# Where quantised tiles stand among VectorE's work: pinned steps, other homes for the tiles, gating in four portions

## The chip, the cores and the metric

The kernel runs on one core of a Trainium2 chip. The core has five engines that work side by side, each with a queue of its own that it works through in order: TensorE (PE in the profile; its weight loads are listed as PEld), VectorE (DVE), ScalarE (ACT), GpSimd (POOL) and SyncE (SP, which here only issues DMA transfers). An engine whose next instruction waits for another engine stands still, and everything behind that instruction in its queue stands with it. The metric is the device time of one execution in microseconds; the time of a kernel is the median of several executions.

## The reference, cut to what matters

Two batches of 4096 tokens with 512 channels pass through two layers, each of which adds an attention part and a feed-forward part to x. In layer 0 the feed-forward part is a product of two tensors that are first quantised: every run of 32 numbers in a row shares a scale, and each number divided by the scale is rounded to a 6-bit grid.

```python
xn = _layernorm(x)
# layer 0, attention: x1 = xn@w1.T+b; conv over 3 tokens, silu, a linear recurrence over all
# tokens (16 states a channel); v = silu(xn@v1.T+b); result (ssm * v) @ w2.T + b
# layer 0, ffn:
xq, xs = _mx_quantize(xn)          # scales = max|block of 32| / 7.5 ; q = nearest on grid
wq, ws = _mx_quantize(weight)
ffn = (xq * xs) @ (wq * ws).T + bias
x = x + attention + ffn
xn = _layernorm(x)
# layer 1, attention: q, k = relu(xn@Wq.T+bq), relu(xn@Wk.T+bk); v = xn@Wv.T+bv;
#   linear attention over 16 heads (sums of k and of k*v over all tokens), + xn, layernorm
# layer 1, ffn: sigmoid(xr@W_r.T) * (relu(xk@W_k.T)**2 @ W_v.T), xr, xk mixes with the token before
x = x + attention + ffn
```

## The kernel before, in words

A block is 512 tokens (T); a batch has NB = 8 of them, and a block has four tiles of 128 tokens (TJ = 4). Channels come in four chunks of 128 (CC = 4). Everything is float32; larger products are made from seven smaller ones instead of eight, with sums and differences made by VectorE and GpSimd beforehand.

The order of the work, with the times at which it lies in the profiled execution:

1. The w1 loops (to about 460 us): `projected` for all 16 blocks makes x1 and v by w1 and v1 and runs the convolution; tables for the recurrence are made beside it. Blocks 13 and 14 go together, by `projected_pair`.
2. The recurrence over tokens (460 to 570), which leaves its result y in memory.
3. For each batch: `mixed`, the w2 loops (570 to 905 for batch 0, from 1430 for batch 1). For each block, "gating" (`gated`) loads four chunks of y and of v, transposes y (L638) and multiplies (L639); TensorE multiplies the gated block by w2 and the quantised tiles by the quantised weight `w_d` into the same bank. Blocks 0 and (in batch 0) 1 go by `branch` and `x1_of` (matmuls L743, sums L751), the later ones by `x1_by_seven` (matmuls L787, sums L805). Then follow the layer norm of the result, its transposed form xnT and the keys of layer 1 (L902, L903).
4. `outer_sums` (905 to 982 us for batch 0), the product of keys and x over all tokens, one block in about 12 us: VectorE makes four differences (L951) and GpSimd eight (L943), TensorE multiplies (L971).
5. `pairs` (982 to 1175): q and the feed-forward keys for two blocks at a time (matmuls L1081).
6. `layer1` (1175 to 1430): attention, the second feed-forward product and the output, block by block. It calls `at_block(i, half)` in each block, a place for work that belongs to the next batch.

**A quantised tile** is 128 tokens, 64 of them in all, and four more for the weight. `quantised` is a generator in four steps: load xq (a DMA on SyncE's queue, L456); rescale it (four ScalarE activations, L136), take the scales (VectorE: L187, L188, L192) and multiply (GpSimd, L193); round by a conversion to FP8 (VectorE, L201) and multiply by the scales (GpSimd, L202); transpose (VectorE, L464) and, unless the tile goes straight to a place on the chip, store it. `stepped(tiles)` is what the loops call at chosen places: it takes the first tile in the list a step further, and the second as well once the first has done more than two. A tile therefore goes through in about two calls. Its buffer xq comes from the pool "yv" of eight buffers, which y and v of the gating use too, unless it is given another home.

Where the tiles stand before:

- the w1 loops (`beside`): blocks 0 to 5 of batch 0 (24 tiles) and the weight's four;
- the w2 loops (`tiles` in `mixed`): blocks 6 and 7 of the batch at hand (8 tiles), stepped in the branch loop, in `x1_of(0)`, in `x1_by_seven` and in the loop of the keys;
- the outer sums of batch 0 (`early`): blocks 4 and 5 of batch 1 (8 tiles), one call at every second item;
- the pairs of batch 0 (`later`): blocks 1 to 3 of batch 1 (12 tiles), one call at each of the places that `seven` offers;
- layer 1 of batch 0 (`ahead`): block 0 of batch 1 (4 tiles).

The gating of block 0 of batch 1 stands in layer 1 of batch 0 too, all four chunks at `at_block(7, 0)`.

**What sets the order.** The program is written as a sequence of steps, but a scheduler of the framework places each engine's instructions, from what each depends on and its own view of when they will be ready. So an engine's queue can differ from the order in which the instructions are written. The call `tc.keep_in_program_order(ins)` holds an instruction behind the one that was traced before it on its engine; it changes the place in the queue and adds no instruction.

Of the kernel before, what the change touches and what calls it, by code (L numbers as in the profile page):

```python
# [13 lines left out]
ALU = mybir.AluOpType  # L14
# [3 lines left out]
P = 128  # L18
# [26 lines left out]
def block_kernel(ctx: ExitStack, tc: tile.TileContext, a: dict, out: bass.AP):  # L45
# [132 lines left out]
    def laid_normalised(y, mv, rescaled=rescaled):  # L178

        for h in range(QC):  # L180
            part = y.rearrange("p (c h q) -> p c h q", h=QC, q=QB)[:, :, h, :]
            rescaled(part, part, mv[:, h, :])

    def mx_scaled(y):

        s = small.tile([P, NQ], F32, tag="mx_s", name="mx_s", bufs=6)
        nc.vector.tensor_reduce(s, by_block(y), AX.X, ALU.max, apply_absolute_value=True)  # L187
        nc.vector.tensor_scalar(  # L188
            s, s, (1.0 / 7.5) / GRID, 1e-30 / GRID, ALU.mult, ALU.max
        )  # L190
        rs = small.tile([P, NQ], F32, tag="mx_rs", name="mx_rs")
        nc.vector.reciprocal(rs, s)  # L192
        nc.gpsimd.tensor_tensor(  # L193
            by_block(y), by_block(y), rs.unsqueeze(2).to_broadcast([P, NQ, QB]), ALU.mult
        )
        return s

    def mx_rounded(y, s):

        q = small.tile([P, D], FP8, tag="mx_q", name="mx_q")  # L200
        nc.vector.tensor_scalar(q, y, -LOWER * GRID, None, ALU.add, saturate=False)  # L201
        nc.gpsimd.tensor_tensor(  # L202
            by_block(y), by_block(q), s.unsqueeze(2).to_broadcast([P, NQ, QB]), ALU.mult
        )
# [184 lines left out]
            :, 2 * j : 2 * j + 2, half * 2 * P : (half + 1) * 2 * P  # L389
        ]  # L390

    def projected_pair(work, m, xa, xb, before, sums):

        x_work = lambda name: work.tile([P, T], F32, tag="x", name=name, bufs=10)
        ts = [None] + [[x_work("t") for _ in range(2)] for _ in range(3)]
# [38 lines left out]
        for half in range(2):  # L434
            seven(
                two_quarters(half), sums[half], lambda k: xa[:, k, :], lambda k: xb[:, k, :], ts,
                ("acc", "mm", "tr"), partial(put, half), lambda: None,
                held=[x_work("held") for _ in range(4)],
            )
        return x1s[1]  # L440

    def quantised_weight(o):
        y = yv.tile([P, D], F32, tag="yv", name="w_y")
        nc.sync.dma_start(out=y, in_=a["ffn_w"][o])
        yield
        s = mx_scaled(y)
        yield
        mx_rounded(y, s)
        yield
        nc.vector.transpose(wd[:, :, o * P : (o + 1) * P], y)  # L450
        yield

    def quantised(n, j, dst, temp, home=None):

        xq = home("xq") if home else yv.tile([P, D], F32, tag="yv", name="xq")
        nc.sync.dma_start(out=xq, in_=a["xi"][n * TJ + j])  # L456
        yield
        laid_normalised(xq, mvi[:, :, n, j, :])
        scales = mx_scaled(xq)
        yield  # L460
        mx_rounded(xq, scales)
        yield
        xd = dst().rearrange("p c t -> p (c t)") if dst else temp()
        nc.vector.transpose(xd, xq)  # L464
        if not dst:
            nc.sync.dma_start(out=xqd[n, j], in_=xd)
        yield
# [173 lines left out]
    def mixed(b, z0, xds, xnTs, mvs, w2, wk, outer):  # L641
# [19 lines left out]
        def at(time, do):  # L661
            events[max(time, clock[0])].append(do)

        tiles = [
            quantised(b * NB + m, j, None, t2q) for m in (NB - 2, NB - 1) for j in range(TJ)
        ]

        def xnT_of(i):
# [64 lines left out]
        def x1_of(i):  # L733

            xt, z = xts[i], zs.pop(i)
            for j in range(TJ):
# [15 lines left out]
                nc.sync.dma_start(out=xd1[b * NB + i, j * P : (j + 1) * P], in_=xt[:, j, :])  # L752
                tick()
                gate(i + 1, j)
                if i == 0:
                    stepped(tiles)
            measured_x1(i, xt)

        def halves_of(z, xd):
# [107 lines left out]
        for i in range(plain):  # L867

            pos[i] = [bank(("mm", "tr")[i]) if j < 2 else acc() for j in range(TJ)]
            for j in range(TJ):  # L870
                branch(i, j, pos[i][j])
                if i == 0:
                    tick()
                stepped(tiles)
        x1_of(0)
        w_sums = [weight_sums(quarters(w)) for w in (wd, w2)]
        xd_read(2)
# [324 lines left out]
    def layer1(b, xrs, mvs, kvx, wts, at_block):  # L1202
# [143 lines left out]
        loaded(0)  # L1346
        for i in range(NB + 1):
            steps = receptance(i) if i < NB else iter(())
            if i < NB:
                at_block(i, 0)  # L1350
            if i + 1 < NB:
                loaded(i + 1)
            for j in range(TJ):
                next(steps, None)
                if i:
                    added(i - 1, j)
                if j < TJ - 1:
                    next(steps, None)
                if i < NB:
                    attention(i, j)  # L1360
                    if j == 1:
                        at_block(i, 1)
            if i < NB:
                normalised(i)

# [6 lines left out]
    with tc.tile_pool(name="tab", bufs=1) as tab:  # L1372
# [3 lines left out]
        with pool("a", 2) as work, pool("pm", 1) as pm:  # L1376
# [32 lines left out]
            for u in range(2):  # L1409
# [17 lines left out]
                    m, j, partial(homes[m], j) if m in homes else None,  # L1427
                    lambda: work.tile([P, D], F32, tag="xe", name="c"),
                )
                for m in range(NB - 2)  # L1430
                for j in range(TJ)
            ]
            beside += [quantised_weight(o) for o in range(CC)]
# [11 lines left out]
            while n < NK:  # L1445
                if n == PAIRED:

                    xi = laid(work, n + 2)
                    x1 = projected_pair(work, n, xnT, xnT_b, x1, sums)
# [53 lines left out]
    for b in range(B):  # L1503
# [5 lines left out]
        early, later = [], []  # L1509
        if b + 1 < B:  # L1510
            tile_of = lambda m, j, home=None: quantised((b + 1) * NB + m, j, None, t2q, home)
            early = [tile_of(m, j, t2) for m in (4, 5) for j in range(TJ)]
            later = [tile_of(m, j) for m in range(1, 4) for j in range(TJ)]
        for n, item in enumerate(outer):
            if n % 2:
                stepped(early)
            gt = item
        while early:
# [89 lines left out]
```

## Time and profile before

| | |
|---|---|
| runs shown, us | 2279.46, 2282.87, 2285.77 |
| median, us | 2282.87 |
| profiled execution, us | 2286.98 |
| its span, us | 2285.2 |
| mean granted clock of TensorE | 0.997 |
| TensorE busy, us | 2233.7 (98% of the span), 8032 matmuls |
| VectorE busy, us | 1589.7 (70%), 3115 instructions |
| ScalarE busy, us | 1052.0 (46%), 2066 instructions |
| GpSimd busy, us | 543.5 (24%), 576 instructions |

The profile is of one execution; "L639" is line 639 of the kernel before. Groups of instructions are named `out<-in` by the tiles that they write and read. An idle time is put down to what ended it: `[8.64 <-DVE x L805]` is 8.64 us in which the engine stood, until VectorE's instruction of line 805 that writes x was done. The granted clock is the share of full speed that TensorE was given in a stretch. A stretch in the windows view shows the busy time of TensorE, of its weight loads, of VectorE, ScalarE and GpSimd, then the granted clock, the share of the DMA engines and GB/s.

### The profile page before, as it was taken

How to read it: one execution, taken by the hardware profiler on the slowest of the kernel's cores; microseconds unless marked ns; L12 is line 12 of the kernel's file. 1: busy time of each engine (PE TensorE's matmuls, PEld its weight loads, DVE VectorE, ACT ScalarE, POOL GpSimd, SP SyncE). 2: the span in 40 equal slices, each digit the busy share in tenths (PEclk: the TensorE clock that was granted, in tenths of full speed). 3: DMA queues.
4: the chain of work that ended last, by engine and by line, in shares of the span. 5: the costliest groups of instructions: out<-in, count | busy, mean ns of one | idle time of the engine just before them, and what ended most of it. 6: DMA issues, size and time to landing. Idle time of an engine off the chain costs nothing. (4 is left out here: it accounts for less than half of the span.)

```text
span 2285.2 us, 25778 instructions
## 1 busy us (share of the span) xinstructions
PE 2233.7 (98%) x8032; PEld 1337.0 (59%) x8032; DVE 1589.7 (70%) x3115; ACT 1052.0 (46%) x2066; POOL 543.5 (24%) x576
## 2 busy tenths in 40 slices
PE   7999999999999999999999999899999999999999
PEld 3443344455467676854456665567676864456665
DVE  6798847655676764588678878776664455558877
ACT  5777884546232234367763332222132256653332
POOL 0124300011342224722021111423233600001111
PEclk9999999999999999999999999999999999999999
DMA  7865543389876557523276788756556412266876
GB/s 252 278 222 157 164 153 114 117 265 320 293 233 221 176 177 224 188 102 137 112 268 164 213 214 244 238 176 218 172 165 208 161 49 81 97 226 155 218 211 167
DMA packets 304571, 431.15 MB, mean 189 GB/s; under 512 B 60081, under 2 KB 121521, under 8 KB 303409
## 3 DMA queue, kind: packets, MB, share of 16 engines
q1 hardware_dynamic: 262096, 330.91, 44.0%
q10 hardware_dynamic: 29088, 67.12, 7.6%
q0 software_dynamic: 13248, 31.46, 7.4%
q8 instruction: 64, 1.05, 0.2%
q14 instruction: 75, 0.61, 0.1%
HBM read 249.42 MB, written 148.53 MB: 174 GB/s over the span
## 5 line engine op out<-in xcount | busy, mean ns | idle before, releaser
L165 PE MATMUL p_acc<-w_W_v,t 128*128 128x512 f32 x512 | 230.2, 594 | 1.2 <-DMA t<-kd 1.2
L1318 POOL DMA_DIRECT2D x<-row_beta x64 | 55.9, 898 | 427.9 <-DVE den L1300 220.3
L165 PEld LDWEIGHTS p_acc<-w_W_v,t 128*128 128x128 f32 x512 | 96.4, 190 | 102.2 <-issue 95.3
L193 POOL TENSOR_TENSOR xq<-xq,mx_rs 128x512 f32<-128x512 f32 x64 | 71.4, 1117 | 330.0 <-DVE mx_rs L192 168.8
L136 ACT ACTIVATE xq<-xq,mvi 128x128 f32<-128x128 f32 x256 | 109.0, 484 | 83.1 <-DMA xq<-in_xi 68.8
L860 POOL TENSOR_TENSOR ksum<-ksum,k 128x512 f32<-128x512 f32 x62 | 84.8, 1367 | 257.0 <-ACT k L903 249.9
L903 ACT ACTIVATE k<-k 128x512 f32<-128x512 f32 x64 | 40.3, 630 | 209.6 <-DVE k L902 180.1
L485 DVE SCALAR_TENSOR_TENSOR xc<-x,col_conv_w,xc 128x512 f32<-128x512 f32 x128 | 99.1, 796 | 41.7 <-ACT x L346 23.6
L165 PE MATMUL p_acc<-xnT,w_w_w 128*128 128x512 f32 x224 | 103.8, 607 | 5.1 <-ACT x L364 2.3
L118 ACT ACTIVATE rs_s<-rs_v 128x4 f32<-128x4 f32 (+1 forms) x41 | 8.4, 206 | 211.9 <-DVE rs_v L116 211.7
L787 PE MATMUL p_mm<-w_sums,t 128*128 128x256 f32 x416 | 96.9, 387 | 8.6 <-DVE x L805 8.6
L165 PE MATMUL p_acc<-xnT,w_v_w 128*128 128x512 f32 x224 | 101.2, 594 | 3.2 <-ACT v L380 3.1
L165 PE MATMUL p_acc<-w_Wk,xnT 128*128 128x512 f32 x224 | 101.5, 593 | 1.2 <-DVE xnT L697 1.2
L165 PE MATMUL p_tr<-w_Wk,xnT 128*128 128x512 f32 x224 | 100.9, 592 | 0.0
L131 DVE BATCH_NORM_STATS2 st<-x 128x6 f32<-128x512 f32 x128 | 83.7, 677 | 22.7 <-DMA x<-in_x 21.8
L136 ACT ACTIVATE xi<-xi,mvi 128x128 f32<-128x128 f32 x208 | 89.3, 483 | 11.1 <-DMA xq<-in_xi 3.7
L787 PE MATMUL p_acc<-w_sums,t 128*128 128x256 f32 x416 | 94.2, 379 | 0.0
L787 PEld LDWEIGHTS p_mm<-w_sums,t 128*128 128x128 f32 x416 | 80.9, 195 | 21.0 <-DVE x L805 9.3
L136 ACT ACTIVATE t<-t,mvj 128x128 f32<-128x128 f32 x224 | 87.6, 479 | 3.5 <-DMA ktd<-k 3.1
L971 PE MATMUL p_acc<-t,t 128*128 128x256 f32 x384 | 88.1, 379 | 0.0
L202 POOL TENSOR_TENSOR xq<-mx_q,mx_s 128x512 f32<-128x512 fp8e4 x64 | 72.3, 1130 | 64.5 <-DVE mx_q L201 39.2
L1081 PE MATMUL p_acc<-x,w_sums 128*128 128x512 f32 x192 | 85.3, 593 | 0.5 <-ACT t L1088 0.5
(317 smaller groups left out, 5096.0 us busy)
## 6 DMA issues: line engine op xcount, KB each, us to landing
x<-in_x SPq DMA_DIRECT2D x126, 256.0 KB, 5.6
xq<-in_xi SPq DMA_DIRECT2D x64, 256.0 KB, 3.6
vd<-v ACTq DMA_DIRECT2D x64, 256.0 KB, 2.6
cd<-xs SPq DMA_DIRECT2D x64, 256.0 KB, 2.1
xg<-cd SPq DMA_DIRECT2D x16, 1024.0 KB, 8.3
v<-vd SPq DMA_DIRECT2D x64, 256.0 KB, 5.2
xd<-x SPq DMA_DIRECT2D x64, 256.0 KB, 2.2
ktd<-k SPq DMA_DIRECT2D x64, 256.0 KB, 2.2
```

The source lines that it names most:

```text
L131: nc.vector.bn_stats(st[:, j, :], xt(j))
L136: nc.scalar.activation(dst, src, AF.Identity, bias=mv[:, 0:1], scale=mv[:, 1:2])
L165: nc.tensor.matmul(out_ap, lhsT=lhsT(k), rhs=rhs(k), start=(k == 0), stop=(k == CC - 1))
L193: nc.gpsimd.tensor_tensor(by_block(y), by_block(y), rs.unsqueeze(2).to_broadcast([P, NQ, QB]), ALU.mult)
L202: nc.gpsimd.tensor_tensor(by_block(y), by_block(q), s.unsqueeze(2).to_broadcast([P, NQ, QB]), ALU.mult)
L485: nc.vector.scalar_tensor_tensor(xc, x1[:, tap : tap + T], conv_w[:, cc, tap : tap + 1], xc, ALU.mult, ALU.add,)
L787: nc.tensor.matmul(po[:, u * 2 * P : (u + 1) * 2 * P], lhsT=x(k)[:, c, u, :], rhs=w(k)[:, c, :], start=first and k == 0 and c == 0 and u == 0,
L860: nc.gpsimd.tensor_tensor(ksum, ksum, kt, ALU.add)
L903: nc.scalar.activation(kt, kt, AF.Relu)
L971: nc.tensor.matmul(pg[name][:, c * HW : (c + 1) * HW], lhsT=x(u)[:, c * P : (c + 1) * P], rhs=k(u), start=(i == 0 and u == 0 and c == 0), ...
L1081: nc.tensor.matmul(banks[c], lhsT=lhsT(k, c), rhs=rhs(k), start=first and k == 0, stop=k == 1, skip_group_check=True,)
L1318: nc.gpsimd.dma_start(out=x[:, j, :], in_=beta, accum_op=ALU.add)
```

## The change

Four things are altered; what is computed stays the same.

1. The reduce (L187), the conversion to FP8 (L201) and the transpose (L464, and the weight's) are pinned in program order on VectorE.
2. The w2 loops of a batch have only its last block's four tiles, not eight, and step them neither in the branch loop nor in `x1_of(0)`: the first call comes in `x1_by_seven` or the loop of the keys. Block 6 of batch 0 goes to the w1 loops (28 tiles there), and `projected_pair` gets the calls too.
3. The tiles of batch 1, blocks 1 to 6 (24 of them), stand in one order: the first 13 in the pairs of batch 0, the other 11 in the outer sums, which come earlier in time. In the outer sums the call stands at three of four items.
4. The gating of batch 1's block 0 is dealt out over four calls of `at_block`: (7, 0), (7, 1), (8, 0) and (8, 1), one chunk at each.

```diff
+    in_order = tc.keep_in_program_order
+
     def mx_scaled(y):
         s = small.tile([P, NQ], F32, tag="mx_s", name="mx_s", bufs=6)
-        nc.vector.tensor_reduce(s, by_block(y), AX.X, ALU.max, apply_absolute_value=True)
+        in_order(
+            nc.vector.tensor_reduce(s, by_block(y), AX.X, ALU.max, apply_absolute_value=True)
+        )
...
     def mx_rounded(y, s):
         q = small.tile([P, D], FP8, tag="mx_q", name="mx_q")
-        nc.vector.tensor_scalar(q, y, -LOWER * GRID, None, ALU.add, saturate=False)
+        in_order(nc.vector.tensor_scalar(q, y, -LOWER * GRID, None, ALU.add, saturate=False))
...
-    def projected_pair(work, m, xa, xb, before, sums):
+    def projected_pair(work, m, xa, xb, before, sums, between):
...
-                held=[x_work("held") for _ in range(4)],
+                partial(between, m, 0), [x_work("held") for _ in range(4)],
...
-        nc.vector.transpose(wd[:, :, o * P : (o + 1) * P], y)
+        in_order(nc.vector.transpose(wd[:, :, o * P : (o + 1) * P], y))
...
-        nc.vector.transpose(xd, xq)
+        in_order(nc.vector.transpose(xd, xq))
...
         tiles = [
-            quantised(b * NB + m, j, None, t2q) for m in (NB - 2, NB - 1) for j in range(TJ)
+            quantised(b * NB + NB - 1, j, None, t2q) for j in range(TJ)
         ]
...
                 gate(i + 1, j)
-                if i == 0:
-                    stepped(tiles)
             measured_x1(i, xt)
...
                 if i == 0:
                     tick()
-                stepped(tiles)
         x1_of(0)
...
-            if i < NB:
-                at_block(i, 0)
+            at_block(i, 0)
...
-                    if j == 1:
-                        at_block(i, 1)
+                if j == 1:
+                    at_block(i, 1)
...
-                for m in range(NB - 2)
+                for m in range(NB - 1)
                 for j in range(TJ)
...
-            early = [tile_of(m, j, t2) for m in (4, 5) for j in range(TJ)]
-            later = [tile_of(m, j) for m in range(1, 4) for j in range(TJ)]
+            order = [(m, j) for m in range(1, NB - 1) for j in range(TJ)]
+            later = [tile_of(m, j) for m, j in order[:13]]
+            early = [tile_of(m, j, t2) for m, j in order[13:]]
         for n, item in enumerate(outer):
-            if n % 2:
+            if n % 4 != 2:
                 stepped(early)
             gt = item
...
-            if b + 1 < B and (i, half) == (NB - 1, 0):
-                next_in.append(t8())
-                for cc in range(CC):
-                    gated(b + 1, 0, next_in[0], cc)
+            cc = 2 * (i - NB + 1) + half
+            if b + 1 < B and cc >= 0:
+                if cc == 0:
+                    next_in.append(t8())
+                gated(b + 1, 0, next_in[0], cc)
```

More of the change, by code (lines that the diff above doesn't have):

```diff
@@ L1448, in block_kernel @@
                     xi = laid(work, n + 2)
-                    x1 = projected_pair(work, n, xnT, xnT_b, x1, sums)
+                    x1 = projected_pair(work, n, xnT, xnT_b, x1, sums, between)
                     xnT = turned(work, n + 2, xi, rescaled_by_dve)
```

## The prediction

> **What bounds the kernel now.** First the busy times of the page:
>
> ```profile
> PE 2233.7 (98%) x8032; PEld 1337.0 (59%) x8032; DVE 1589.7 (70%) x3115; ACT 1052.0 (46%) x2066; POOL 543.5 (24%) x576
> ```
>
> TensorE works 2233.7 of 2285.2 us. Neither its matmuls nor their number change, so all that the change can win is the idle 51.5 us and the matmuls that ran at a lower granted clock after idling; all that it can lose is new idle time. So the waits of TensorE come second (line, what it waited for, us in total, times, longest us):
>
> ```profile
> PE p_mm L787 <- DVE x L805: 10.2, 2, 8.6
> PE p_tr L159 <- DVE xn L313: 9.2, 1, 9.2
> PE p_tr L743 <- DVE t L639: 3.5, 2, 2.2
> ...
> PE p_mm L1235 <- DVE rs_e L122: 1.7, 1, 1.7
> PE p_acc L1235 <- DVE t L1227: 1.7, 1, 1.7
> PE p_acc L1081 <- DVE k L1133: 1.6, 1, 1.6
> ```
>
> The 9.2 is the kernel's start, which stays. The longest is at the start of batch 1; here is the timeline there (start, duration):
>
> ```profile
> 1457.72 3.62 PE L787 MATMUL p_acc<-w_sums,t 128*128 128x256 f32 x16
> 1466.75 0.43 DVE L201 TENSOR_SCALAR mx_q<-xq 128x512 fp8e4<-128x512 f32 x1
> 1469.25 0.68 DVE L805 TENSOR_TENSOR x<-x,p_mm 128x512 f32<-128x512 f32 x1
> 1469.98 6.52 PE L787 MATMUL p_mm<-w_sums,t 128*128 128x256 f32 x16 [8.64 <-DVE x L805]
> ```
>
> TensorE has done its product at 1461.34 and stands until VectorE's L805 has emptied the bank. VectorE isn't idle then: it works down its queue, in which steps of quantised tiles (L201 and others) stand ahead of L805. The same sixteen matmuls take 3.62 us before the stall and 6.52 after it, the granted clock being 0.50 to 0.54 in that stretch: 2.90 us more. Batch 0's start:
>
> ```profile
> 587.13 2.25 SPq L456 DMA_DIRECT2D xq<-in_xi  x4
> 589.70 0.33 SPq L635 DMA_DIRECT2D y<-yd  x1
> 612.23 3.60 PE L743 MATMUL p_tr<-w_w_w,t 128*128 128x512 f32 x4 [2.17 <-DVE t L639]
> ```
>
> Four tiles' loads take freed "yv" buffers on SyncE's queue before the y and v of block 1's gating (L635 to L639), and w2's products wait for that gating. And the end of layer 1 of batch 0, where L639 of batch 1's first gating stands ahead of the sums L1227:
>
> ```profile
> 1385.05 0.69 DVE L639 TENSOR_TENSOR t<-t,v 128x512 f32<-128x512 f32 x1 [1.90 <-DMA v<-vd]
> 1387.79 1.99 PE L1235 MATMUL p_acc<-w_sums,t 128*128 128x256 f32 x8 [1.68 <-DVE t L1227]
> ```
>
> **Gains, part by part.**
>
> *Fewer tiles in the w2 loops.* Between the first weight sum (1410.06) and L805 (1469.25), VectorE has 54.9 us of work in the 59.2 us. In the changed order 44.4 us stand between the same two; the 10.5 gone are steps of some five tiles (one is 0.67 + 0.22 + 0.24 + 0.48 + 0.70 = 2.3 us by the rows of L187, L188, L192, L201, L464). With the 4.3 us of waits kept, L805 comes at 1410.1 + 44.4 + 4.3 = 1458.8, and it can't come before its product ends at 1457.9. It is needed at 1461.3. So the 8.64 go, and 0.8 of a later short wait in the same loop and 2.90 of clock: 12.3. Next late is the rstd chain of the same block, which L805 also stands behind in the queue; I leave 1 us for it and take 11.3 (bounds 5 and 12.3).
> Batch 0: without loads of tiles in the branch loop, y and v have the buffers at once, and the gating ends before 604.9, when TensorE needs it. 2.17 and 1.33 of wait go, and 3.60 − 1.88 = 1.7 of clock (1.88 is what the same four take at 618.24): 5.2. I take 4.7 (0 to 5.2). That the clock fell here after a wait of 2.17 us is this trace's row.
> On that row, the Trainium skill ("TensorE: Matmul & The Clock Gate", "What's actually happening") has the half rate set in only after an idle window of about 3.4 us. By it the short stall would cost no clock and the gain would be 3.5, not 5.2; the row disagrees, with 0.71 granted in 610 to 615 us, and I go by the row.
>
> *Gating in four portions.* The y and v loads and the eight VectorE instructions (four times 0.70 + 0.67) remain, two halves of a block apart. In the changed order the first portion stands behind L1227's sums, and no xq load lies between y and v on SyncE. The 1.68 and 1.70 go; I take 3.0 (0 to 3.4), since the later portions stand in the last blocks of layer 1, where TensorE's longest wait on ScalarE is 0.8.
>
> Gains: 11.3 + 4.7 + 3.0 = 19.0 us.
>
> **Costs, part by part.** The same 64 tiles are stepped; what left the w2 loops goes to three other places.
>
> *The pins.* They add no instruction. They hold a step behind what was traced before it, so a tile is a chain: reduce, two small ones, POOL's L193 (1.05 at the least, 1.12 mean), L201, POOL's L202 (1.13), transpose. Where nothing else stands between, VectorE waits about 1.1 us twice a tile: 4.4 us instead of 2.3. Behind the waiting L201 stands whatever is traced next. Counting in the two orders the work between a tile's neighbouring steps, and 1.2 us less that work as the wait, VectorE's waiting for POOL grows from 32.6 to 67.6 us. Much of it is covered: VectorE has 45% free in the w1 loops after 300 us and some 35% in batch 0's keys, and in layer 1 a tile's steps stand about 17 us apart, so POOL is long done. It counts in three places.
>
> *Outer sums of batch 0 (905 to 982 us): 11 tiles instead of 8.* TensorE has a block of 12.1 us, almost without idle time. VectorE and POOL side by side before:
>
> ```profile
> 945.43 1.82 DVE L951 TENSOR_TENSOR t<-t 128x512 f32<-128x512 f32 x2
> 947.17 1.21 DVE L951 TENSOR_TENSOR t<-t,t 128x512 f32<-128x512 f32 x1
> 948.93 0.64 DVE L951 TENSOR_TENSOR t<-t,t 128x512 f32<-128x512 f32 x1
> 938.90 0.43 DVE L201 TENSOR_SCALAR mx_q<-xq 128x512 fp8e4<-128x512 f32 x1 [1.22 <-POOL xq L193]
> ```
>
> Three tiles in a block give POOL 3 × 2.14 + 8 × 0.82 (L943) = 13.0 us, over 12.1; VectorE gets 3 × 2.3 + 4 × 0.92 (L951) = 10.6, plus POOL waits. Laid out by hand in the changed order from 909.3 with these durations, block 6's last L951 comes at 964.7 where TensorE needs it at 961.7, and POOL's last sum of block 7 at 977.8 where 976.8 (then shifted by the first) would do: 3 + 1 = 4 us. Least: 0, if L951 slips into each wait. Most: no overlap, 3 × 4.4 + 3.7 = 16.9 us a block, 4.8 over, in 11/3 blocks: 17.6. I take 4, as the hand layout has the order.
> On the L951 rows, the skill's "SBUF — State Buffer" ("Who interferes with whom") speaks against the change: a VectorE operation with two inputs in SBUF and a GpSimd operation that reads SBUF lock each other out whole. The trace shows L951 at 1.21 beside L943 and at 0.64 alone, so a loss of 0.57. By the rule each of the six added POOL multiplies could hold one L951 for its full 1.05, 6 us; by the row 3.4.
>
> *Pairs of batch 0 (982 to 1100): 13 tiles instead of 12.* VectorE is 89% busy in the worst stretch, and TensorE waits 2.1 us there:
>
> ```profile
> 1000.00:1050.00 50.00, 47.89 (x116) 21.05 (x116) 44.65 (x85) 34.28 (x63) 14.06 (x12) 1.00 0.38 140
> ```
>
> (The columns: TensorE, weight loads, VectorE, ScalarE, POOL.) The changed order spreads the tiles later, behind the k's, but with two uncovered waits each: 2.3 more work and some 8 us more of waiting against 5.4 + 10.3 us free up to 1100. I take 3.5 (0 if the later place frees the worst stretch, 8 if all the waiting shows).
>
> *w1 loops (150 to 350): 28 tiles instead of 24.* Four more cost ScalarE 4 × 4 × 0.48 = 7.8 us and VectorE 9.2; they run at about 310 to 340 us, where VectorE is busy 27.4 of 50 and TensorE idles for nothing, but ScalarE is busy 40.4. The earlier ones, pinned, act on a stretch where TensorE idles 7.6 us already (2.7, 2.8 and 2.0 in 150 to 300). I take +1 (−2 to +6). The paired blocks' step is a call that finds no tiles left: nothing. The loads keep their number.
>
> Costs: 4 + 3.5 + 1 = 8.5. **Sum: −19.0 + 8.5 = −10.5 us.** The profiled execution took 2286.98 (span 2285.2 and 1.8 around it), so 2276.5 on that base. It lies 4.1 above the median of the runs shown, so beside 2282.87 I forecast 2272.4.
>
> **The rivals.**
> A. *The covers hold.* For: where tiles stand in a queue with slack, as in layer 1, TensorE shows no wait on L201 or L464 at all. Against: POOL's 13.0 against 12.1. Costs then 0 to 1: −18.5, 2264.
> B. *The stalls move instead of going.* L805 comes at 1458.8 by the sum, but behind the fourth L751 stand statistics, ScalarE's root and four small steps; from L751 at 1464.70 to L805 took 4.55 us, 2.3 of it tile steps. If the last L751 comes only at 1462 instead, L805 is at 1464.3, a stall of 3 and its clock of about 2. Gains 14, costs 10 to 14: −2, 2281.
> C. *Slower: the tile chain in the outer sums.* If VectorE and POOL don't overlap there, the term is 17.6 us, and four stalls of about 4 us each halve the clock after them; by 1.7 us each, 6.8 more. −19 + 17.6 + 6.8 + 4.5 = +10: 2293. It decides from 14.5 us on in that stage (19 less the other 4.5), a block of 16 us. Against: L951 ran between tile steps at 945 to 950 without a wait.
>
> **How the numbers follow.** The forecast 0.53, its own range 2265 to 2279; A 0.17; B 0.16; C 0.14. A change under 0.3% (6.8 us) can hardly be told from none here. Faster: 0.48 of the forecast's 0.53, A's 0.17, 0.02 of B: 0.67. Same: 0.05 + 0.11 of B + 0.02 of C: 0.18. Slower: 0.15. The range runs from 2261 (A with −1 in the w1 loops, and some more) to 2289 (half-way from B to C), leaving out half of C and a little of A.
>
> **What would show it.** Right: TensorE's wait on L805 at the start of batch 1 under 1 us with 3.6 us for the sixteen matmuls after it; no wait on L639 in batch 0's first blocks; none on L1227 before the gating of batch 1. Costs: a wait of L971 on L951 or L943 near 961 and 974 us of 3 to 4 us in all; VectorE's wait of L201 on L193 up from 30.5 to some 50 us or more. Wrong: TensorE's idle total not near 40 us, or new waits of L165 on VectorE in the w1 loops.

## The result, and the profile after

The changed kernel takes 2315.65 us (median of four runs, 2312.13 to 2316.25) beside 2283.66 before: the ratio is 1.0139, with a 95% interval of 1.0121 to 1.0157. It is slower by 32 us, where 10 us of gain were forecast, and outside the range that was given.

Its profiled execution has a span of 2314.1 us, 28.9 more than before. The page's busy line:

```profile
PE 2242.6 (97%) x8032; PEld 1340.5 (58%) x8032; DVE 1599.4 (69%) x3115; ACT 1052.9 (45%) x2066; POOL 551.3 (24%) x576
```

TensorE's idle time went from 51.5 to 71.5 us (span less busy), and the same 8032 matmuls took 8.9 us more, at a lower clock after idling. No other engine's work grew by more than 10 us. TensorE's waits (line, what it waited for, us in total, times, longest):

```profile
PE p_acc L165 <- DMA t<-kd: 13.6, 7, 5.4
PE p_tr L159 <- DVE xn L317: 9.2, 1, 9.2
PE p_mm L1082 <- DVE q L1125: 6.3, 2, 3.7
PE p_acc L165 <- DVE xnT L337: 5.4, 2, 3.2
PE p_mm L165 <- ACT v L384: 3.9, 3, 1.9
PE p_tr L1292 <- DVE t L1303: 3.0, 1, 3.0
PE p_mm L972 <- ACT xg L136: 2.9, 2, 2.2
PE p_acc L165 <- DVE mv L124: 2.5, 1, 2.5
PE p_tr L972 <- DVE t L952: 2.4, 1, 2.4
```

The waits on L805 and on L639 are gone from the list. New or longer ones stand in the w1 loops (L165 on L337, which was 1.8 us before, on L384 and L124), the outer sums (L972), the pairs (L1082), and in layer 1, where the second product waits for the load of kd (13.6 us, 1.2 before).

Since both kernels run the same instructions, a trace can be laid beside that of the kernel before: the lag is how much later an instruction starts than the same one there (VectorE's instructions that read a product, median over 25 us). The growth of the lag over a stage is what the stage lost (+) or won (−), in us. Each row is one execution. This table is the backbone of all that follows:

| kernel | w1 loops | start, batch 0 | outer sums | pairs | layer 1, batch 0 | start, batch 1 | to the end |
|---|---|---|---|---|---|---|---|
| forecast | +1 | −4.7 | +4 | +3.5 | −3 | −11.3 | 0 |
| after | +13.8 | −6.8 | +9.5 | +10.5 | +10.8 | −11.6 | +3.2 |
| e1 pins only | +6.4 | −4.0 | +1.4 | +9.6 | +13.6 | −3.6 | +1.7 |
| e2 no pins | −3.6 | −1.0 | +7.0 | +0.3 | −1.4 | −3.3 | +4.1 |
| e3 gating only | +0.7 | −0.8 | +0.4 | −0.1 | +4.0 | +4.3 | +0.8 |
| e4 no pins in w1 | −2.7 | −6.9 | +10.5 | +9.4 | +11.1 | −10.4 | +0.3 |
| e5 pins in w2 only | +1.1 | −6.8 | +7.0 | +0.3 | +0.3 | −11.3 | +1.2 |
| e6 and 8 in outer | +0.8 | −7.4 | +0.2 | +2.1 | +4.6 | −10.3 | +1.5 |
| e7 and gating at once | −2.4 | −7.2 | +0.4 | +2.2 | +3.4 | −16.7 | +3.4 |
| e8 late calls only | 0.0 | +5.1 | +0.5 | 0.0 | +0.5 | −3.7 | +0.6 |
| e9 e7, layer 1 pinned | +2.3 | −6.6 | +0.5 | +0.7 | +13.4 | −16.7 | +0.7 |
| e10 w1 loads by GpSimd | +20.8 | −7.1 | +9.8 | +9.2 | +11.4 | −10.3 | +0.7 |
| e11 late and pinned | −0.9 | −6.9 | +0.5 | 0.0 | +0.9 | −15.9 | +1.3 |
| e12 w1 own buffers | +5.0 | −7.7 | +10.4 | +9.4 | +11.1 | −13.0 | +1.6 |
| e13 w1 transposes free | +5.1 | −6.6 | +10.5 | +9.5 | +11.4 | −10.3 | +3.5 |

How fine it is can be read off it: the w1 loops of e2, e4, e5, e6, e7 and e9 are the same code, and came out between −3.6 and +2.3. So 3 us in one cell mean little there; the last column is batch 1's layer 1, where the change alters nothing, and varies from 0.3 to 4.1. The edge between layer 1 and the start of batch 1, at about 1425 us of the kernel before, lies inside the last 32 matmuls of layer 1's second product, so a wait in front of them is shared out over both cells.

What the lost stages look like after the change, from TensorE's timelines (start, duration, the wait before it):

```profile
972.45 3.58 PE L972 MATMUL p_tr<-t,t 128*128 128x256 f32 x8 [2.38 <-DVE t L952]
985.97 4.52 PE L972 MATMUL p_mm<-t,xg 128*128 128x256 f32 x12 [2.18 <-ACT xg L136]
...
1075.71 3.70 PE L1082 MATMUL p_mm<-x,w_Wq 128*128 128x512 f32 x8 [2.65 <-DVE q L1125]
1130.17 6.65 PE L1082 MATMUL p_mm<-x,w_Wq 128*128 128x512 f32 x8 [3.69 <-DVE q L1125]
...
1384.01 6.03 PE L165 MATMUL p_acc<-w_W_v,t 128*128 128x512 f32 x8 [5.44 <-DMA t<-kd]
```

The first two are the outer sums (the eight matmuls took 1.89 before), then the pairs, then layer 1; in the last two stages such eight take 3.60 without a wait. The pairs' two waits and the clock after the second, 2.65 + 3.69 + 3.05, are 9.4 of the 10.5 us that this stage lost. And the start of batch 1, where sixteen matmuls now follow sixteen without a wait:

```profile
1497.40 3.62 PE L789 MATMUL p_acc<-w_sums,t 128*128 128x256 f32 x16
1500.86 3.62 PE L789 MATMUL p_mm<-w_sums,t 128*128 128x256 f32 x16
```

### The profile page after: what moved, and what is told of

It reads as the page before. It is cut to its first block, busy times and chain, and to the rows that moved or that the text cites. A ratio compares the mean times of both kernels' runs of the same rounds, so it can differ in the third digit from the quotient of the medians.

```text
span 2314.1 us, 25726 instructions
## 1 busy us (share of the span) xinstructions
PE 2242.6 (97%) x8032; PEld 1340.5 (58%) x8032; DVE 1599.4 (69%) x3115; ACT 1052.9 (45%) x2066; POOL 551.3 (24%) x576
## 5 line engine op out<-in xcount | busy, mean ns | idle before, releaser
L165 PE MATMUL p_acc<-w_W_v,t 128*128 128x512 f32 x512 | 234.2, 603 | 13.6 <-DMA t<-kd 13.6
L165 PEld LDWEIGHTS p_acc<-w_W_v,t 128*128 128x128 f32 x512 | 98.3, 194 | 117.2 <-issue 97.2
L165 PE MATMUL p_acc<-xnT,w_w_w 128*128 128x512 f32 x224 | 104.8, 612 | 9.6 <-DVE xnT L337 5.4
L206 POOL TENSOR_TENSOR xq<-mx_q,mx_s 128x512 f32<-128x512 fp8e4 x64 | 78.0, 1219 | 113.1 <-DVE mx_q L205 102.5
L165 PE MATMUL p_acc<-xnT,w_v_w 128*128 128x512 f32 x224 | 101.1, 594 | 0.9 <-ACT v L384 0.9
L165 PE MATMUL p_acc<-w_Wk,xnT 128*128 128x512 f32 x224 | 100.7, 592 | 0.0
L165 PE MATMUL p_tr<-w_Wk,xnT 128*128 128x512 f32 x224 | 100.7, 592 | 0.0
L783 POOL TENSOR_TENSOR x<-x,row_w_b 128x512 f32<-128x512 f32 x52 | 71.6, 1401 | 84.4 <-DMA x<-in_x 49.8
L972 PE MATMUL p_acc<-t,t 128*128 128x256 f32 x384 | 88.1, 379 | 0.0
L1082 PE MATMUL p_acc<-x,w_sums 128*128 128x512 f32 x192 | 85.4, 593 | 1.6 <-ACT t L1089 1.6
```

The lines of the kernel that those rows point to most:

```text
L165: nc.tensor.matmul(out_ap, lhsT=lhsT(k), rhs=rhs(k), start=(k == 0), stop=(k == CC - 1))
L206: nc.gpsimd.tensor_tensor(by_block(y), by_block(q), s.unsqueeze(2).to_broadcast([P, NQ, QB]), ALU.mult)
L783: nc.gpsimd.tensor_tensor(xt[:, j, :], xt[:, j, :], b_out, ALU.add)
L972: nc.tensor.matmul(pg[name][:, c * HW : (c + 1) * HW], lhsT=x(u)[:, c * P : (c + 1) * P], rhs=k(u), start=(i == 0 and u == 0 and c == 0), ...
L1082: nc.tensor.matmul(banks[c], lhsT=lhsT(k, c), rhs=rhs(k), start=first and k == 0, stop=k == 1, skip_group_check=True,)
```

## The experiments

**The parts apart.** Theory 1 was that the pinned chains are the cost, theory 2 that the numbers of tiles are.

*e1: the kernel before, with the pins.* The edit is the `in_order` lines of the diff, nothing else:

```diff
+    in_order = tc.keep_in_program_order
...
-        nc.vector.transpose(xd, xq)
+        in_order(nc.vector.transpose(xd, xq))
```

> The kernel before with nothing but the pins. By stages the whole change lost 13.8 us in the w1 loops, 9.7 in the outer sums, 10.4 in the pairs, some 9 in layer 1 of batch 0 and won 6.9 and 11.6 at the starts of the two batches. Theory 1 (the chain of a pinned tile is the cost): w1 loops +10 to +14 with 24 tiles already, pairs +7 to +10, outer sums +3 to +6, starts of the batches unchanged or worse; 2300 to 2315 us. Theory 2 (the number of tiles in a place is the cost, and order within a tile is free): within 4 us of 2283.

Measured: 2311.35 beside 2285.69, ratio 1.0110 (1.0091 to 1.0129). The pins alone make most of the loss: 9.6 us in the pairs and 13.6 in layer 1 with as many tiles as before. In the w1 loops they cost 6.4, less than expected.

*e2: the whole change without the pins.*

```diff
-    in_order = tc.keep_in_program_order
+    in_order = lambda ins: ins
```

> The whole change without the pins: tiles in the new places, gating in four portions. Theory 1 (the chain): the losses of w1 loops, outer sums and pairs shrink to a third or less, the gains at the starts of the batches stay; 2262 to 2278 us. Theory 2 (the number of tiles): as the whole change, 2308 to 2318 us.

Measured: 2292.44, ratio 1.0028 (1.0015 to 1.0040). Neither number came: the losses of w1 loops, pairs and layer 1 are gone as theory 1 has it, but the outer sums keep 7.0, so that loss belongs to the 11 tiles and their pace. And the gains at the starts shrink to −1.0 and −3.3, from −6.8 and −11.6: the rest needs the pins. The wait on the sum that empties the bank is back:

```profile
1468.45 5.97 PE L789 MATMUL p_mm<-w_sums,t 128*128 128x256 f32 x16 [5.48 <-DVE x L807]
```

*e3: the kernel before, with the gating in four portions.* The edit is the parts of the diff in `layer1` and `at_block`:

```diff
-            if b + 1 < B and (i, half) == (NB - 1, 0):
...
+            cc = 2 * (i - NB + 1) + half
+            if b + 1 < B and cc >= 0:
+                if cc == 0:
+                    next_in.append(t8())
+                gated(b + 1, 0, next_in[0], cc)
```

> The kernel before with nothing but the gating in four portions. The forecast had 3 us won at the end of layer 1 of batch 0; in the changed kernel that layer lost some 9 us, most of it waits of the second product (L165) on the load of kd. Theory 1 (the gating has no part in it, the loads of kd vary): 2278 to 2283 us, no wait on kd over 1 us. Theory 3 (the portions of gating are the cause, by their loads or by their place on VectorE): layer 1 loses 5 to 10 us, 2286 to 2292 us, waits on kd of 5 us and more in sum.

Measured: 2293.73, ratio 1.0036 (1.0022 to 1.0051). Theory 3 holds, 2 us beyond its range: 4.0 lost in layer 1, and 4.3 more at the start of batch 1. TensorE's waits there:

```profile
PE p_mm L787 <- DVE x L805: 12.0, 3, 10.3
...
PE p_acc L165 <- DMA t<-kd: 5.7, 5, 3.5
```

*e4: the whole change, unpinned in the w1 loops.*

```diff
+    pinned = []
-    in_order = tc.keep_in_program_order
+    in_order = lambda ins: tc.keep_in_program_order(ins) if pinned else ins
...
             while beside:
                 stepped(beside)
+            pinned.append(True)
```

> The whole change with the pins from batch 0's w2 loops on only, so that the 28 tiles and the weight's four in the w1 loops go unpinned. Theory 1 (the chain): the 13.8 us of the w1 loops fall to 0 to 4, all later stages as in the whole change; 2301 to 2306 us. Theory 2 (four more tiles there): 2313 to 2317 us.

Measured: 2298.44, ratio 1.0052 (1.0033 to 1.0071), somewhat faster than expected. The w1 loops go from +13.8 to −2.7 with 28 tiles, and the other stages repeat those of the whole change within about 1.5 us, the last column apart. So four more tiles cost nothing there as long as they are not pinned. But the pins with 24 tiles cost 6.4 (e1), not 13.8: some 7 us take both, the pins and the four tiles more.

**Pins where they win.** e5 to e7 build on each other; e8 takes the forecast's mechanism alone.

*e5: the whole change, pinned in the w2 loops only.*

```diff
+    pinned = [False]
-    in_order = tc.keep_in_program_order
+    in_order = lambda ins: tc.keep_in_program_order(ins) if pinned[0] else ins
...
+        pinned[0] = True
         ksum = mixed(b, z0, xds, xnTs, mvs, *c_wts, outer)
+        pinned[0] = False
```

> The whole change, but pinned in the w2 loops only, where the starts of the batches lie; the tiles of the w1 loops, outer sums, pairs and layer 1 unpinned. By stages the unpinned form had -4 in the w1 loops, -1 and -3 at the two starts, +7 in the outer sums, 0 in the pairs, -1 in layer 1, +4 in the second layer 1; the pinned form -7 and -12 at the starts. Theory 1 (pins win in the w2 loops and lose elsewhere): the sum of the better ones, -4 -7 +7 0 -1 -12 = -17, with up to +4 in layer 1 of batch 1; 2267 to 2276 us beside 2285. Rival (the gains at the starts are not due to the pins in the w2 loops, but to the later state that the earlier pins leave): as unpinned, 2288 to 2293 us.

Measured: 2279.41, ratio 0.9974 (0.9963 to 0.9985). The gains at the starts return in full (−6.8 and −11.3) with pins in these loops alone, and pairs and layer 1 lose nothing. The time is 3 us above what was expected, nearest to the w1 loops (+1.1 where −4 was set down).

*e6: e5 with 8 tiles in the outer sums.*

```diff
-            later = [tile_of(m, j) for m, j in order[:13]]
-            early = [tile_of(m, j, t2) for m, j in order[13:]]
+            later = [tile_of(m, j) for m, j in order[:16]]
+            early = [tile_of(m, j, t2) for m, j in order[16:]]
...
-            if n % 4 != 2:
+            if n % 2:
```

> As the one pinned in the w2 loops only, with 8 tiles in the outer sums, a call at every second item as before, and 16 in the pairs. If the 11 tiles and their pace cost the 7 to 10 us of the outer sums, this stage goes back to within 1 us of before, and the pairs take four more tiles for 0 to 3 us: 5 to 9 us below the one with 11. If the pairs are full, they lose what the outer sums win: equal within 3 us.

Measured: 2275.48, ratio 0.9953 (0.9937 to 0.9968). The outer sums are back at +0.2, from +7.0. The pairs take 16 tiles, unpinned, for 2.1 us. Layer 1 gives some back (+4.6), so the sum fell by 4 us, less than expected.

*e7: e6 with the gating of batch 1's block 0 at once.* The reverse of e3's edit in `at_block`:

```diff
-                gated(b + 1, 0, next_in[0], cc)
...
+                for cc in range(CC):
+                    gated(b + 1, 0, next_in[0], cc)
```

> As the one with 8 tiles in the outer sums, with the gating of batch 1's block 0 at once, as before. If the portions help (the forecast's 3 us), this is 2 to 4 us slower, with waits of 1.7 us on L1227's sums back. If they hurt, by y and v loads ahead of the load of kd, it is 3 to 8 us faster.

Measured: 2271.99, ratio 0.9940 (0.9920 to 0.9960): 3.5 us below e6, on the side where the portions hurt. It shows at the start of batch 1: −16.7 rather than −10.3. The last wait of layer 1 in e6 and then in e7:

```profile
1405.05 0.39 SPq L1346 DMA_DIRECT2D out<-x  x1
1405.53 0.42 SPq L101 DMA_DIRECT2D w_Wk<-in_Wk  x1
1406.00 2.45 SPq L1331 DMA_DIRECT2D t<-kd  x1
1415.84 16.31 PE L165 MATMUL p_acc<-w_W_v,t 128*128 128x512 f32 x32 [4.21 <-DMA t<-kd]
```

```profile
1397.92 0.39 SPq L1346 DMA_DIRECT2D out<-x  x1
1400.81 0.38 SPq L101 DMA_DIRECT2D w_Wk<-in_Wk  x1
1403.44 0.36 SPq L1331 DMA_DIRECT2D t<-kd  x1
1409.64 14.00 PE L165 MATMUL p_acc<-w_W_v,t 128*128 128x512 f32 x32 [0.18 <-DMA t<-kd]
```

On SyncE's queue the load of kd stands behind the store `out<-x`, which waits for its last sums, and a load of the weight Wk. With the portions that store comes 7.1 us later. The issue of kd's load begins only 2.6 later, though, which is no more than e6 as a whole is behind there (2 to 3 us). What differs is what stands close in front of it: in e6 store, weight (1 MB) and kd (1 MB) are issued within 1 us, in e7 over 5.5 us. In e6 the load then takes 2.45 us to issue rather than 0.36, and is there 9.8 us after its issue began rather than 6.2. TensorE waits 4.21 us rather than 0.18 and then runs the 32 matmuls in 16.31 rather than 14.00 us: 4.0 + 2.3 = 6.3, of the 7.6 by which the cells of layer 1 and of the start of batch 1 together differ. In e3 kd's load is issued 1.2 us earlier than in the kernel before (1407.87 against 1409.05), 0.47 behind the weight's rather than 2.63, and lands after 9.4 us rather than 6.2; TensorE waits 3.49 us and then takes 16.74 for the 32, with nothing but the portions changed. That the portions' work on VectorE makes the store late is what the places suggest; it was not tried apart, and neither was the order of the two loads.

*e8: the kernel before, without the early calls, nothing pinned.*

```diff
                 gate(i + 1, j)
-                if i == 0:
-                    stepped(tiles)
             measured_x1(i, xt)
...
                 if i == 0:
                     tick()
-                stepped(tiles)
         x1_of(0)
```

> The kernel before, with only the calls in the branch loop and in the first block's w2 loop taken away: eight tiles still in the w2 loops, nothing pinned, tiles and gating elsewhere as before. The forecast's mechanism alone (tile steps ahead of L805, tile loads ahead of y and v): -5 at the first start, -11 at the second: 2268 to 2272 us beside 2285. Rival (without pins the scheduler puts steps of later tiles ahead of L805 all the same): gains of 2 to 5 us in all, a wait on L805 of 4 us or more stays.

Measured: 2289.07, ratio 1.0011 (1.0000 to 1.0022). The rival holds, and more: in sum nothing is won. The two waits on L639 are gone, but batch 0 then loses 5.1 us in the loops that follow, and at batch 1, where 3.7 are won, the wait for the most part only changes its form:

```profile
1460.39 3.53 PE L785 MATMUL p_mm<-w_d,t 128*128 128x256 f32 x8 [2.70 <-DVE x L751]
1473.52 5.41 PE L785 MATMUL p_mm<-w_sums,t 128*128 128x256 f32 x16 [4.26 <-DVE x L803]
```

Where a step is called does not settle where it stands in the queue: between 1461 and 1470 us two tiles' steps still stand on VectorE ahead of the L803 at 1472.79, for which TensorE waits.

**Layer 1.** *e9: e7 with the four tiles of layer 1 pinned too.*

```diff
+        pinned[0] = True
         layer1(b, xnTs, mvs, kvx, [load_weight(s) for s in ("W_r", "W_v")], at_block)
+        pinned[0] = False
```

> The best form so far (pins in the w2 loops, 8 tiles in the outer sums, gating at once) with the four tiles of layer 1 pinned too. With pins everywhere layer 1 of batch 0 lost 11 to 14 us, without them it lost or won a few. Theory A (a pinned step on VectorE holds POOL's multiplies, behind which POOL issues the accumulating stores that the load of kd waits for on SyncE): layer 1 loses 6 to 12 us more than in the best form; 2278 to 2284 us. Theory B (the loss in layer 1 was carried in from the pairs, by tiles left there late): within 3 us of the best form, 2270 to 2275 us.

Measured: 2278.39, ratio 0.9971 (0.9962 to 0.9980), 6.4 us above e7; layer 1 loses 13.4 in place of 3.4 in the executions that were traced. Theory A's size holds: four pinned tiles, 9.2 us of work on VectorE, cost some 10 us, and nothing need be carried in from the pairs. GpSimd's waits in layer 1 have an entry that is there when layer 1's tiles are pinned (e9 here; 16.0 in e1, 15.9 in the changed kernel) and not in the kernel before, e2, e7 or e11:

```profile
POOL xq L198 <- DVE mv L132: 16.0, 4, 5.0
```

These are the tile's multiplies waiting for VectorE. But the entry shows two things at once, since unpinned the four tiles don't run in layer 1 at all. GpSimd's first multiply of each tile begins between 1147 and 1170 us in the kernel before, and between 1145 and 1167 in e7, at the end of the pairs; the scheduler has moved them there. In e9 the four begin between 1215 and 1311. The pin holds the tile in the stage where it is written, and no run tells this apart from the waiting within a tile.

Nor does theory A's path, from the multiplies by GpSimd's transfers to the store and to kd, show at the longest wait. SyncE and TensorE there, in e9 and then SyncE at the same place in e7:

```profile
1342.13 0.39 SPq L1346 DMA_DIRECT2D out<-x  x1
1342.62 0.41 SPq L640 DMA_DIRECT2D y<-yd  x1
1343.13 0.65 SPq L642 DMA_DIRECT2D v<-vd  x1
1343.87 0.43 SPq L640 DMA_DIRECT2D y<-yd  x1
1344.40 0.37 SPq L642 DMA_DIRECT2D v<-vd  x1
1344.86 0.38 SPq L1331 DMA_DIRECT2D t<-kd  x1
1355.25 5.46 PE L165 MATMUL p_acc<-w_W_v,t 128*128 128x512 f32 x8 [6.30 <-DMA t<-kd]
```

```profile
1338.25 0.39 SPq L1346 DMA_DIRECT2D out<-x  x1
1339.55 0.37 SPq L1331 DMA_DIRECT2D t<-kd  x1
```

The store comes 3.9 us later than in e7 and kd's issue 5.3 later, where e9 is 4.7 behind there anyway: neither is late by more than 0.6. But four loads of y and v, 1 MB together, have come to stand between them, and kd's load lands 10.4 us after its issue rather than 5.8. The wait of 6.30 and the slower eight matmuls after it (5.46 for 3.60) are 8.2 of the 10 us. All seven kernels whose tiles in layer 1 are pinned (the changed one, e1, e4, e9, e10, e12, e13) have these loads right ahead of one load of kd, which lands 9.3 to 11.0 us after its issue; the others don't have them there. So what these traces show as the carrier is the load's neighbours on SyncE's queue. Why the pins bring them there was not tried.

**The w1 loops.** Here ScalarE is held up too. Its first waits in 150 to 320 us, in the kernel before and then in the changed one:

```profile
ACT xc L483 <- DVE xs L494: 13.2, 12, 4.9
ACT xc L492 <- DVE xc L485: 11.8, 9, 2.8
```

```profile
ACT xq L136 <- DMA xq<-in_xi: 19.6, 12, 4.5
ACT xc L496 <- DVE xc L489: 14.5, 11, 2.6
```

ScalarE also makes w1's and v1's evictions (L368, L384), which stand behind a tile's rescaling. e4, unpinned there, doesn't have the first entry. What makes the loads late was asked three times.

*e10: the whole change, these loads issued by GpSimd.*

```diff
-        nc.sync.dma_start(out=xq, in_=a["xi"][n * TJ + j])
+        (nc.sync if by_sync else nc.gpsimd).dma_start(out=xq, in_=a["xi"][n * TJ + j])
```

> The whole change, pins everywhere, with the loads of the w1 loops' tiles issued by GpSimd in place of SyncE. In the w1 loops SyncE stands 43.9 us before the stores of tiles (15.5 before the change), with the next tile's load behind them, ScalarE then waits 19.6 us for loads of tiles (none of that before), with the evictions of w1's products behind. Theory S (SyncE's queue carries the delay on): ScalarE's wait falls under 6 us and the w1 loops lose 3 to 8 us rather than 13.8; 2305 to 2310 us. Theory V (VectorE, held by the chain, is itself what TensorE waits for, whatever the loads do): the w1 loops still lose 11 us or more; 2312 us and over.

Measured: 2320.01, ratio 1.0143 (1.0126 to 1.0160); w1 loops +20.8, ScalarE's wait 29.5. Theory S's number did not come, but SyncE's queue is not cleared by that: the loads now stand in GpSimd's queue among the multiplies, and wait there for earlier tiles' transposes (31.3 us in 16 waits between 150 and 320 us), one of them here:

```profile
208.18 0.56 POOL L460 DMA_DIRECT2D xq<-in_xi  x1 [1.58 <-DVE c L468]
```

*e12: the whole change, six buffers of their own for these tiles.*

```diff
-        with pool("a", 2) as work, pool("pm", 1) as pm:
+        with pool("a", 2) as work, pool("pm", 1) as pm, pool("xw", 6) as xw:
...
                     lambda: work.tile([P, D], F32, tag="xe", name="c"),
+                    lambda name: xw.tile([P, D], F32, tag="xw", name=name),
```

> The whole change, pins everywhere, where the tiles of the w1 loops have six buffers of their own instead of what is left of the eight shared ones (four of which hold the turned tiles of block 0). With the loads on GpSimd each load still waited for the transpose of an earlier tile, so the buffer, not SyncE's queue, may be what makes loads late. Theory B (buffers come free late, because the pinned transposes are late): ScalarE's wait for loads of tiles in 150 to 320 us falls from 19.6 to under 6 us, and the w1 loops lose 2 to 8 us rather than 13.8; 2303 to 2310 us. Theory V (the chain on VectorE and the engines that wait for it, whatever the buffers): ScalarE's wait falls or not, the w1 loops lose 10 us or more; 2311 us and over.

Measured: 2304.93, ratio 1.0076 (1.0053 to 1.0100); w1 loops +5.0. *e13: the whole change, the transposes of the w1 loops not pinned.* The list `late` is empty until these loops are over.

```diff
+    turned_in_order = lambda ins: in_order(ins) if late else ins
...
-        in_order(nc.vector.transpose(xd, xq))
+        turned_in_order(nc.vector.transpose(xd, xq))
```

> The whole change, where in the w1 loops the reduce and the conversion are pinned and the transposes are not. Theory B (late transposes hold the buffers and with them the loads): the w1 loops lose 0 to 5 us, ScalarE's wait for loads of tiles is under 8 us; 2302 to 2308 us. Theory V (any pinned step that waits for GpSimd makes VectorE wait, and what stands behind it): half of the loss or more stays, 7 to 13 us; 2309 to 2315 us.

Measured: 2309.29, ratio 1.0098 (1.0069 to 1.0127); w1 loops +5.1.

Both take 9 us off the stage, as theory B has it. But ScalarE's wait for the loads hardly moves (18.9 and 20.3), against theory B. In e12 these loads still follow a tile's store on SyncE, and SyncE stands 38.6 us in front of such stores (43.9 in the changed kernel): own buffers together with loads on another queue were not tried, so theory S stays open for this wait. With e1 (24 tiles, +6.4, a wait of 14.9) this divides the 13.8: some 5 to 6 go with every pinned form that was run; some 9 take pinned transposes, shared buffers and the four tiles more together, and go when any one of the three is taken away. What TensorE then no longer waits for is VectorE's L337 and L124 in e12 (5.7 us in that stretch of the changed kernel); in e13 a wait on L339 of 4.6 stays, so the path of the 9 us is not settled.

**A version that beats both.** *e11: the kernel before with e8's edit and the pins, switched as in e5 to the w2 loops alone.*

```diff
+        pinned[0] = True
         ksum = mixed(b, z0, xds, xnTs, mvs, *c_wts, outer)
+        pinned[0] = False
```

> The kernel before with two edits: no calls in the branch loop and in the first block's w2 loop, and the pins for the tiles of the w2 loops alone. Tile numbers elsewhere (24, 8, 12, 8) and the gating as before. If late calls and pins together are what wins at the starts of the batches, both gains are there (-7 and -11 to -16) and every other stage is within 3 us of before: 2262 to 2268 us, ratio 0.990 to 0.993. If four tiles fewer in these loops are needed too, a wait on L805 of 3 us or more stays at one of the starts: 2271 to 2280 us.

Measured: 2264.86 beside 2285.09, ratio 0.9905 (0.9890 to 0.9920). Both starts are won (−6.9 and −15.9) and no other stage moves by more than 1.3. TensorE's waits, first four:

```profile
PE p_tr L159 <- DVE xn L318: 9.1, 1, 9.1
PE p_acc L165 <- ACT v L385: 3.3, 4, 1.4
PE p_acc L165 <- DMA t<-kd: 2.2, 4, 1.4
PE p_acc L165 <- DVE xnT L338: 1.9, 1, 1.9
```

Neither four tiles fewer in these loops, nor the other homes, nor the portions are needed for it.

## Why the prediction was wrong

The gains at the starts came, the third gain did not, and all the costs were too small. By the forecast's own terms:

*Fewer tiles in the w2 loops.* 11.3 and 4.7 were forecast; 11.6 and 6.8 came. That 11.6 lies so near 11.3 is luck: where the gating is at once, 16 to 17 us go at batch 1, above the bound of 12.3, and the portions take some 5 back. The stall and its price were read rightly: the 16 to 17 are 8.64 + 0.81 + 2.90, the second short wait on L805 of 1.6 (10.2 − 8.6 in the list of waits) and some 2 us more. But the cause was put in the wrong part of the change. I ascribed it to fewer and later calls; e8 shows that later calls alone lose 5.1 at one start and win 3.7 at the other, and e1 that the pins alone win 4.0 and 3.6. It takes both, and fewer tiles are not needed (e11). The order of the changed kernel, from which the 44.4 us were counted, had the pins in it. One reading was off without effect: in the 59.2 us before L805 VectorE is busy 52.8 and idle 6.4 by the window's sums, where the forecast has 54.9 of work and 4.3 of waits.

*Gating in four portions.* Forecast: 3.0 won. By itself it loses 8.3 (e3). The 1.68 and 1.70 do go in e3, but a wait of 2.29 on L1302 and the 3.49 on kd come in their place; the step "the later portions stand in the last blocks of layer 1, where TensorE's longest wait on ScalarE is 0.8" asked about the wrong thing. What is next late there is the load of kd, which lands 9.4 us after its issue rather than 6.2, on a queue that I had not followed.

*Outer sums.* Forecast 4, bounds 0 to 17.6; measured 9.5. The stage was right, and the size less than half of what came: 7.0 belong to the number and pace of the tiles (e2, e5; back to 0.2 with 8 in e6), some 2.5 to the pins. The lateness forecast for the last two blocks came as a wait of 2.38 us on VectorE, and of 1.50 on GpSimd before it. A third, of 2.18, is on ScalarE, which waited 9.18 us for a load of xg that stood on SyncE behind the store of a tile:

```profile
977.46 4.84 SPq L470 DMA_DIRECT2D xqd<-mx_c  x2
982.39 0.88 SPq L926 DMA_DIRECT2D xg<-xd  x2
985.11 0.81 ACT L136 ACTIVATE xg<-xg,mvs 128x512 f32<-128x512 f32 x1 [9.18 <-DMA xg<-xd]
```

The forecast's layout had VectorE and GpSimd in it, not this queue. The clock after the waits of 2.38 and 2.18 took 1.7 (3.58 for 1.89) and 1.8 (4.52 for 2.75), which the sum of 4 had left out, though the forecast's own rival C counted it.

*Pairs.* Forecast 3.5, bounds 0 to 8; measured 10.5, and 9.6 with pins alone and one tile fewer. 16 unpinned tiles cost 2.1 (e6), with layer 1's four moved in beside them. The step that failed is "8 us more of waiting against 5.4 + 10.3 us free": free time anywhere in 100 us was set against waits that fall in front of single evictions.

*w1 loops.* Forecast +1, bounds −2 to +6; measured +13.8. The four tiles, on which the term was built, cost nothing unpinned (e4); pins alone cost 6.4 (e1), and pins with the four tiles 13.8. The forecast had the pins' chain in view, and called it covered from 300 us on, where VectorE has 45% free. TensorE's matmuls, compared as in the table, are 9.6 us behind by 300 us, where the share free was known to be small, and 4.2 more are lost from there to 400, in what was called covered.

*Layer 1.* Costed at nothing, because "POOL is long done" when VectorE takes a tile's next step. Measured +10.8, and e9 gives some 10 of it to four pinned tiles. The cover was named for the wrong direction: VectorE doesn't wait for GpSimd there, GpSimd waits for VectorE (16 us). And rival A's "as in layer 1" had no tiles of this stage to go by, since before the change the scheduler had moved the four to the end of the pairs. Most of the loss is one wait of 5.44 us on kd and the slower eight matmuls after it (6.03 for 3.60): 7.9 of the 10.8. That load has four other loads ahead of it on SyncE's queue, as in e9.

So the rule of the sum, a wait counts where its own engine is full, was wrong. VectorE's waiting for GpSimd in tiles grew about as counted: its five entries that begin with mx_q or the transpose of xq sum to 46.3 us before and 75.1 after, 29 more where 35 were counted from the orders. The waits were counted; where they fall, and what the pins do to the transfers' places, was not followed. In the pairs they fall ahead of single evictions on VectorE itself (L1125), in layer 1 and the outer sums the longest or last waits are for loads on SyncE's queue, and in the w1 loops a part goes by ScalarE. Rival C had the sign but the wrong place: outer sums without overlap would have cost 17.6, and they did overlap. Rival B did not come; L805 was in time.

## What to carry to other kernels

Pinning an instruction moves it to where it is written, and that helps only where it had been standing ahead of something urgent; pin those few places, not a helper that is used everywhere. It also holds it in the stage where it is written, where a scheduler may have had a better place. A step with several engines in turn puts its waits into each engine's queue, so ask for every one what stands behind it there, and for every load that TensorE needs what has come to stand in front of it, and not how busy the engine is. When a change has parts that are to work together, run them apart: here one part and a half carried all the gain (e11), and the other parts all the loss.

## What was not expected of the hardware

A short idle time of TensorE may or may not cost clock. After waits of 2.38 and 2.18 us the next matmuls took 1.9 and 1.6 times as long (3.58 for 1.89, 4.52 for 2.75). After one of 2.65 us, in the pairs, eight matmuls of 512 columns took 3.70 us, beside 3.60 without a wait. The last 32 matmuls of layer 1 took 14.00 us after a wait of 3.29 (e2), and 15.70 after one of 2.28 (the changed kernel). All these waits are shorter than the idle window of about 3.4 us that the Trainium skill ("TensorE: Matmul & The Clock Gate", "What's actually happening") gives for the half rate, so these runs agree with it where nothing was lost (2.65 and 3.29) and not in the others. In a forecast the half rate after waits of 2 to 3 us is better put in as a range, from nothing to 2 us each.

A load's time to land went with what was issued just ahead of it; no run moves the one without the rest. The last load of kd in batch 0's layer 1 (1 MB) landed 6.2 to 6.9 us after its issue where the load of the weight Wk (1 MB) was issued 2.6 us before it (the six kernels without the portions), 8.3 where it was issued 2.0 before (the changed kernel), and 9.0 to 9.9 where it was issued 0.5 before (the eight others with the portions).
